# A spectral mixer on one core: 1/std applied at the point of use, no pool change ahead of half 1's first images, mixing by pairs of chunks

## The chip, the cores and the metric

The kernel runs on one core of one Trainium2 chip. The metric is the device time of one execution in microseconds (us); the median over several runs is compared. All data are float32.

## The reference, cut to what matters

The input is an image of 256 x 256 pixels with 128 channels. Layer 0 is a biased attention along the rows; its result x1 (256 tokens of 256 x 128 pixels) goes to layer 1. Layer 1 normalizes tokens, attends over them in a spectral basis, and ends with a mixer of two Fourier layers over groups of four tokens. The change concerns only the mixer:

```
h0  = instance_norm(attn)                                # attn: (64, 4, 256, 128)
h1  = fno_layer(h0, mix_wr[0], ..., norm=True, act=True)
h2  = fno_layer(h1, mix_wr[1], ..., norm=True)
out = instance_norm(h2) + attn
# fno_layer(x): skip = x mixed by a 4x4 matrix, plus a bias
#   xf = irfft2(modes(rfft2(x)) mixed by complex 4x4 weights)   32 x 16 modes
#   if norm: xf = (xf - mean(xf)) / std(xf)
#   y = xf + skip;  gelu(y) if act
```

So each Fourier layer needs the 1/std of the picture that the mixed modes make, per token. That number comes from the energy of the modes, before any picture exists.

## The kernel before, in words

The 256 tokens are worked off in two halves of 128 (a = 0 and 1), tokens or channels on the 128 partitions. A half's picture of 256 x 128 pixels is cut into 16 blocks of 2048 pixels (NB), each of two half-blocks of 1024 (HB). One half's pictures stay on chip (`blocks`, `hb[b]`); the other's go through DRAM (`yd`, `wd`).

The stages of the mixer, for each half:

- `y_blocks` (L1300 on): attention's output picture, 32 units. PE makes it (L1324, L1200), DVE takes it out of PSUM (L1334).
- `first_modes` (L1408 on): modes of the first layer. Scales the modes F, mixes them (`mix_modes`, L1341 on), and synthesizes along the height (`synth_modes`, four chunks c, matmuls at L566 or L576, copies at L584, stores of Gd1 at L589).
- `first_images` (L1452 on): for block b it loads y (L1461, half 1 only) and `gs`, the slices of Gd1 (`load_modes`, L1217, four DMAs of 64 KB). PE makes skip (L1211) and image (L1200) into the tiles `ups`, ACT applies Gelu (L1499); PE transposes the block before it (L1508), computes the statistics of the second skip (`sps`, L1211, then DVE at L1528) and the forward transform along the width (L1531), which goes to DRAM as Yd (L1534). For half 0, `add_w` also writes the residual w to DRAM (L1476 to L1480).
- `second_modes` (L1540 on): loads Yd back as YT in four chunks (L1551), transforms along the height (L1568, copies at L1574), mixes, synthesizes Gd2.
- `output` (L1614 on): per block `h2ps` = skip (L1211) and image (L1200), then ACT's Identity with scale kap and bias c0 (L1621), DVE's addition of w (L1627), and POOL's store to the output (L1628), by half-blocks.

`mix_modes` makes 16 products on DVE (L1358, each over four chunks of 128 tokens, 512 columns), which PE adds up in two PSUM tiles with an identity (L1367). Then come the squares (ACT, L1370), the energy (PE, 16 matmuls `ens`, L1376), 1/sqrt (`rsqrt`, L35 to L43: small DVE operations and one ACT square root), a diagonal (L1387) that PE spreads over all partitions (`rsp`, L1390), a copy (L1396), and two products of 512 columns that put the scaled modes into Z (L1399). Only then does `synth_modes` read Z.

The order of instructions on PE, ACT, DVE, POOL and SP is the program's own (`manual_schedule`), so it is set by Python generators: `weave` runs y_blocks between the steps of first_modes by the amounts of time that each `yield` names. At the end half 0's second modes (m0) alternate with half 1's first modes (m1); then first_images of half 1 runs with the output of half 0 woven in: in step b = 0 to 15, block c = b + 2 of half 0 is output (one step is left out on the way, by the count `due`). In such a step SP issues, in this order: y and gs of half 1's block b + 1; w and gs of half 0's block c + 1; a load that must wait for its buffer holds up all that follow it on SP.

Buffers are tiles of pools; tiles of one tag take turns in `bufs` places. Before, y and w of that stage share the tag `xt` in the pool `op0` with 4 places of 2048 pixels (L1461, L1637). The pools `op0` and `hp1` are opened when `xp` and `mp1`, used by the stages ahead, are closed, and lie over their memory.

Of the kernel before, what the change touches and what calls it, by code (L numbers as in the profile page):

```python
# [512 lines left out]
def layer1(tc, I, C, ident, x1d, upool, U, stats2, mv2, out):  # L513
# [9 lines left out]
    with ExitStack() as ctx:  # L523
# [681 lines left out]
        def skip(ps, src, blk, stop):  # L1205


            for j in range(4):
                for i in range(4):
                    r, o = slice(32 * i, 32 * i + 32), slice(32 * (i ^ j), 32 * (i ^ j) + 32)  # L1210
                    nc.tensor.matmul(rows_of(ps[j][o, :]), blk[r, r], src[r, j], start=True, stop=stop)  # L1211
# [78 lines left out]
        for a in range(2):  # L1290
            h = Half()
            halves.append(h)
            h.col = sp.tile([P, 16], FP, name=f"col_{a}")
            h.bl0 = sp.tile([P, P], FP, name=f"bl0_{a}")
            h.Gd1 = dram.tile([32, 4, 64, P], FP, name=f"Gd1_{a}")
            h.Gd2 = dram.tile([32, 4, 64, P], FP, name=f"Gd2_{a}")
            h.Yd = dram.tile([H, 32, P], FP, name=f"Yd_{a}")
# [43 lines left out]
        def mix_modes(wp, mk, psum, F, l, tag, out, constant=()):  # L1341
# [3 lines left out]
            T, G = P, P // 4  # L1345
            acc = [psum.tile(f"{tag}acc_{r}") for r in range(2)]
            by_c = [z.rearrange("p (c t) -> p c t", c=4) for z in acc]
# [5 lines left out]
            def product(k):  # L1353
                i, x, r, dst = steps[k]
                t = mk("m", [P, 4, G, 4], f"{tag}m_{k}")
                f = F[:, :, x, :].rearrange("p c (g i) -> p c g i", i=4)[:, :, :, i]
                w = mixw[r][:, :, 16 * l + 4 * i : 16 * l + 4 * i + 4]
# [4 lines left out]
            for k, (i, x, r, dst) in enumerate(steps):  # L1362
# [3 lines left out]
                yield 0.6  # L1366
                nc.tensor.matmul(acc[dst], ident, now, start=(i == 0 and x == 0), stop=(i == 3 and x == 1))  # L1367
            sq = mk("f", [P, 2, 4, T], tag + "sq")
            for r in range(2):
                nc.scalar.activation(sq[:, r], by_c[r], AF.Square)  # L1370
            yield 1.8

            en = psum.tile(tag + "ens")
            for c in range(4):
                for r in range(2):
                    nc.tensor.matmul(  # L1376
                        en[:, 0:1], sq[:, r, c, :], om0[:, min(c, 1) : min(c, 1) + 1],
# [3 lines left out]
            rs = wp.tile([P, 2], FP, tag=tag + "rs", name=tag + "rs", bufs=1)  # L1381
            rsqrt(nc, wp, rs[:, 0:1], en[:, 0:1], EPS, "rq")
            left = rs[:, 1:2]
            nc.vector.tensor_mul(left, rs[:, 0:1], rs[:, 0:1])
            nc.vector.tensor_mul(left, left, en[:, 0:1])
            dg = mk("m", [P, P], tag + "dg")
            nc.vector.tensor_scalar(dg, ident, rs[:, 0:1], None, ALU.mult)  # L1387
            yield 1.8
            ps = psum.tile(tag + "rsp")
            nc.tensor.matmul(ps[:, 0:T], ones, dg, start=True, stop=True)  # L1390
            for k, (x, m) in enumerate(constant):
                nc.tensor.matmul(
                    ps[0:1, 256 : 256 + T], x, m, start=(k == 0), stop=(k == len(constant) - 1)
                )
            rsb = mk("m", [P, T], tag + "rsb")
            nc.scalar.copy(rsb, ps[:, 0:T])  # L1396
            Z = mk("f", [P, 4, 2, T], tag + "Z")
            for r in range(2):
                nc.vector.tensor_tensor(Z[:, :, r, :], by_c[r], bc(rsb, 1, 4), ALU.mult)  # L1399
            if constant:  # L1400
                nc.vector.tensor_copy(Z[0:1, 0, 0, :], ps[0:1, 256 : 256 + T])
            else:
                nc.vector.memset(Z[0:1, 0, 0, :], 0.0)
            nc.vector.tensor_scalar(Z[0:32, 0], Z[0:32, 0], wsyn[0:32, 0:1], None, ALU.mult)
            out[:] = [Z, left]
            yield 1.8

        def first_modes(a, wp, mk, psum, gts):  # L1408
# [34 lines left out]
            z = []  # L1443

            yield from mix_modes(wp, mk, psum, F, 0, f"x{a}", z, ((sig, blk[0]), (ch[:, 2:3], ident)))
            Z = z[0]
            for c in range(4):
                synth_modes(wp, psum.pool, Z, P, h.Gd1, f"g1{a}", turned=True, chunk=c, ptag=psum.tag, gts=gts,
                            queues=(nc.gpsimd, nc.scalar))
                yield 2.7  # L1450

        def first_images(a, wp, yp, psk, pst, first=None):  # L1452
# [5 lines left out]
            def load(b):  # L1458
                if a == 1:
                    ys[b] = yp.tile([P, NB], FP, tag="xt", name=f"y2_{b}")  # L1460
# [28 lines left out]
            for b in range(17):  # L1489
# [4 lines left out]
                if b < 16:  # L1494
# [3 lines left out]
                    for j in range(4):  # L1498
                        nc.scalar.activation(by_turn(hb[b])[:, j], rows_of(ps[j]), AF.Gelu)  # L1499
# [40 lines left out]
        def second_modes(a, wp, mk, psum, gts, yts):  # L1540
# [17 lines left out]
            load(0)  # L1558
            yield 6.0
            if a:  # L1560
                load(1)
            for c in range(4):
# [12 lines left out]
                for k in ((2,), (3,), (), ())[c] if a else ((1,), (2, 3), (), ())[c]:  # L1575
                    load(k)
                if c < 3:
                    yield 4.0
            yield None
            z = []  # L1580
            yield from mix_modes(wp, mk, psum, F, 1, f"z{a}", z)
            Z, left = z
            Fw = mk("m", [P, 2, P], f"Fw_{a}")
            nc.vector.tensor_scalar(Fw, F[:, 0], hw0, None, ALU.mult)
            for c in range(4):
                if c == 2:

                    ps = psum.tile(f"cvps_{a}")
# [11 lines left out]
                yield 2.7  # L1600
# [3 lines left out]
            nc.vector.scalar_tensor_tensor(hv, ps[:, 0:1], 4.0, hv, ALU.mult, ALU.add)  # L1604
            nc.vector.tensor_add(hv, hv, left)
            rsqrt(nc, wp, kap, hv, EPS, "rq")
            nc.vector.tensor_mul(kap, kap, ch[:, 4:5])
            nc.vector.tensor_mul(c0, hm, kap)
# [5 lines left out]
        def output(a, b, gs, w, psk):  # L1614

            kap, c0 = (halves[a].col[:, k : k + 1] for k in (8, 9))
            ps = [psk.tile(f"h2ps_{a}_{b}_{j}") for j in range(4)]
            skip(ps, by_turn(hb[b]), blk[1], False)
# [334 lines left out]
```

## Time and profile before

| | us |
|---|---|
| median of 3 runs (lowest, highest) | 2897.19 (2888.25, 2899.63) |
| the profiled execution | 2898.24 |
| its span | 2896.1 |
| mean granted TensorE clock | 0.948 of full speed |

The stages of the mixer in the span, with what they kept busy:

| stage | from, to (us) | PE busy | DVE busy | DMA, GB/s |
|---|---|---|---|---|
| y_blocks, half 0 | 1903, 2043 | 138.4 | 86.4 | 277 |
| first_modes of half 0 with y_blocks of half 1 | 2043, 2190 | 128.9 | 85.7 | 284 |
| first_images, half 0 | 2190, 2332 | 134.0 | 82.9 | 310 |
| second_modes of half 0, with the last y_blocks | 2332, 2387 | 45.5 | 22.9 | 299 |
| both mixes, both syntheses | 2387, 2468 | 64.8 | 47.8 | 102 |
| first_images of half 1 with output of half 0 | 2468, 2680 | 170.8 | 107.5 | 267 to 368 |
| second_modes, half 1 | 2680, 2765 | 52.9 | 34.0 | 194 |
| output, half 1 | 2765, 2896 | 69.9 | 68.6 | 359 |

How to read it: the busy time of an engine is the sum of its instructions in the window, and a matmul's end is modelled, so a busy PE isn't PE at its peak. In the lines of a timeline the first number is the start, the second how long the group took, then engine, line, operation, output and inputs; what stands in brackets is how long the engine was idle before it, and what released it.

### The profile page before, as it was taken

The page shows a single profiled execution, that of the slowest core. Times are in us where ns is not written, and L with a number is a line of the kernel's source. Part 1 is how long each engine was busy: PE and PEld are TensorE (multiplying, and loading weights), DVE is VectorE, ACT ScalarE, POOL GpSimd, SP SyncE. Part 2 cuts the span into 40 slices and gives each one's busy share as a digit, 9 for nine tenths or more (in the row PEclk, how much of TensorE's full clock was granted, in tenths as well). Part 3 has the DMA queues.
Part 4 walks back from the last instruction along what each step waited for, and adds up shares of the span by engine and source line. Part 5 has one row for each costly group of instructions (what it writes and reads, how often), then busy time and mean ns, then how long its engine had stood idle before and what let it go on. Part 6 is the DMA issues. An engine that isn't in the chain of part 4 may idle for free. (4 is left out here: it accounts for less than half of the span.)

```text
span 2896.1 us, 70186 instructions
## 1 busy us (share of the span) xinstructions
PE 2640.4 (91%) x28524; PEld 1920.0 (66%) x28524; DVE 2007.2 (69%) x3239; ACT 1463.0 (51%) x2844; POOL 1647.4 (57%) x1282
## 2 busy tenths in 40 slices
PE   6799999999999999999999899999889987688664
PEld 6677777777777777777777656778665565354432
DVE  7788888888888888888888744756655545356445
ACT  0477777777777777777777512200004501354132
POOL 0399999999999999999999700200015721111011
PEclk9999999999999999999999999999999998799865
DMA  9421222222222222222222101188888983897598
GB/s 371 160 71 64 69 68 68 70 65 67 70 67 67 67 67 67 67 67 67 68 68 67 42 16 53 42 275 276 267 295 299 317 304 84 273 362 277 187 351 338
DMA packets 240955, 430.02 MB, mean 148 GB/s; under 512 B 26038, under 2 KB 169865, under 8 KB 232312
## 3 DMA queue, kind: packets, MB, share of 16 engines
q1 hardware_dynamic: 200184, 333.24, 34.8%
q0 software_dynamic: 23552, 83.90, 7.7%
q10 hardware_dynamic: 16896, 8.39, 1.1%
q8 instruction: 226, 3.70, 0.6%
q14 instruction: 97, 0.79, 0.1%
HBM read 290.17 MB, written 135.27 MB: 147 GB/s over the span
## 5 line engine op out<-in xcount | busy, mean ns | idle before, releaser
L299 POOL TENSOR_TENSOR e<-e,b1T 128x1024 f32<-128x1024 f32 x256 | 606.7, 2370 | 163.5 <-PE u L348 89.8
L303 POOL TENSOR_TENSOR es<-e 128x512 f32<-128x512 f32 x512 | 639.5, 1270 | 20.1
L281 ACT ACTIVATE sc<-sc,b2T 128x512 f32<-128x512 f32 x512 | 339.0, 662 | 364.6 <-PE sc L272 356.4
L323 DVE RECIPROCAL av<-av 128x256 f32<-128x256 f32 x256 | 452.3, 1767 | 27.2 <-DVE og L322 1.4
L281 ACT ACTIVATE e<-sc,b2T 128x512 f32<-128x512 f32 x512 | 348.7, 681 | 0.0
L294 DVE TENSOR_TENSOR e<-sc,b1T 128x1024 f32<-128x1024 f32 x256 | 311.0, 1215 | 0.0
L272 PE MATMUL sc<-qkT 32*128 32x256 f32 x4096 | 293.6, 400 | 1.3 <-DVE e L294 1.3
L311 PE MATMUL av<-e,v 128*32 128x256 f32 x4096 | 274.7, 385 | 0.5 <-POOL e L299 0.5
L1324 PE MATMUL yps<-xt,mpT 128*128 128x256 f32 x1024 | 244.9, 393 | 21.1 <-DVE yt L1334 12.7
L272 PEld LDWEIGHTS sc<-qkT 32*128 32x128 f32 x4096 | 185.3, 184 | 112.3 <-issue 97.8
L322 DVE SCALAR_TENSOR_TENSOR og<-gate,av 128x256 f32<-128x256 f32 x256 | 107.7, 421 | 190.6 <-PE av L316 190.6
L1324 PEld LDWEIGHTS yps<-xt,mpT 128*128 128x128 f32 x1024 | 194.5, 195 | 59.1 <-DVE yt L1334 16.3
L1338 POOL DMA_DIRECT2D yd<-yt x32 | 17.4, 545 | 346.5 <-DVE yt L1334 346.5
L327 POOL TENSOR_TENSOR x<-xt,bo 128x256 f32<-128x256 f32 x256 | 187.4, 732 | 0.0
L246 PE MATMUL qk<-xnT,wT_wq 128*128 128x256 f32 x512 | 179.5, 432 | 1.7 <-ACT xnT L238 1.7
L252 PEld LDWEIGHTS gv<-wT_wv,kvT 128*128 128x128 f32 x1024 | 155.0, 192 | 13.4
L316 PE MATMUL av<-es,ones 128*32 128x256 f32 x2048 | 157.5, 379 | 2.6 <-POOL es L303 2.5
L333 PE MATMUL wo<-wT_wo,og 128*128 128x128 f32 x1024 | 156.8, 276 | 2.7 <-DVE og L324 2.7
L1621 ACT ACTIVATE blocks<-h2ps,col 128x512 f32<-128x512 f32 x128 | 89.0, 777 | 138.5 <-PE h2ps L1200 130.2
L311 PEld LDWEIGHTS av<-e,v 128*32 128x32 f32 x4096 | 107.0, 109 | 76.1 <-POOL e L299 1.0
L348 PE MATMUL u<-adft,x 128*128 128x129 f32 x1024 | 156.4, 275 | 0.0
L252 PE MATMUL gv<-wT_wv,kvT 128*128 128x128 f32 x1024 | 156.0, 275 | 0.0
(524 smaller groups left out, 5204.6 us busy)
## 6 DMA issues: line engine op xcount, KB each, us to landing
xt<-x1d SPq DMA_DIRECT2D x128, 512.0 KB
xb<-in_x_dram SPq DMA_DIRECT2D x32, 1024.0 KB
xt<-in_x_dram SPq DMA_DIRECT2D x128, 256.0 KB
kt<-in_L_conv_kv_x_dram SPq DMA_DIRECT2D x128, 256.0 KB
x1d<-x SPq DMA_DIRECT2D x256, 128.0 KB
gs<-Gd SPq DMA_DIRECT2D x384, 64.0 KB
yd<-yt POOLq DMA_DIRECT2D x32, 512.0 KB, 5.7
xw<-x1d SPq DMA_DIRECT2D x32, 512.0 KB
```

Source lines behind the costliest of these rows:

```text
L246: nc.tensor.matmul(ps[:, 0:256], wT["wq"], xnT, start=True, stop=True)
L252: nc.tensor.matmul(ps[:, 256 + c * P : 256 + (c + 1) * P], kvT[:, c * P : (c + 1) * P], wT["wv"], start=True, stop=True,)
L272: nc.tensor.matmul(sc[h // 2][:, h % 2, c * 256 : (c + 1) * 256], qkT[p, 256 + c * P : 256 + (c + 1) * P], qkT[p, 0:256], start=True, stop ...
L281: nc.scalar.activation(r["e"][1][:, :, c, :] if hp else z, z, AF.Exp, bias=b2T[:, c, s : s + 1])
L294: nc.vector.tensor_tensor(r["e"][0].rearrange("p h c q -> p (h c q)"), r.pop("sc").rearrange("p h x -> p (h x)"), b1T[:, 0:2].rearrange("p ...
L299: nc.gpsimd.tensor_tensor(e1, e1, b1T[:, 2:4].rearrange("p h c q -> p (h c q)"), ALU.mult)
L303: nc.gpsimd.tensor_tensor(r["es"][hp], e[:, :, 0, :], e[:, :, 1, :], ALU.add)
L311: nc.tensor.matmul(ps[hd, 0:256], r["v"][:, c, hd], r["e"][h // 2][:, h % 2, c, :], start=(c == 0), stop=(c == 1),)
L316: nc.tensor.matmul(ps[32 * h : 32 * h + 32, 256:512], self.ones, r["es"][h // 2][:, h % 2, :], start=True, stop=True,)
L323: nc.vector.reciprocal(rd, rd)
L327: nc.gpsimd.tensor_tensor(r["x1"], r["x"], bc(self.bo, 1, 2), ALU.add)
L1324: nc.tensor.matmul(rows_of(ps[j]), mpT[:, sc, tt], by_turn(xt[:, sc])[:, j], start=(sc == 0), stop=False,)
```

## The change

- `mix_modes` now takes the accumulators and a list of chunks `cs`, and mixes only these. `mixed` copies the unscaled sums into Z (ACT one, DVE the other) and takes the squares. `norm` computes 1/std later and leaves it as a column (`h.col[:, 12:13]`) and as a row spread over the partitions (`h.row`). Synthesis starts from the unscaled Z; `norm` is called after the chunks 0 and 1.
- What made up for that: for the first layer, the scale and the constant go into Gelu as its scale and bias (`h.turn`, one pair of columns for each of the four turned orders j), and the skip's blocks `h.bl0` are divided by the 1/std. For the second, `h.bl0` becomes the skip's blocks divided by it (four operations), and `krs`, the product of kap and 1/std, is Identity's scale.
- `second_modes` transforms the chunks 0 and 1, mixes them, with the transforms of chunks 2 and 3 inside this mix, and then mixes the chunks 2 and 3. Half 1's first modes are stepped along with both.
- The pool `op0` is gone. `hp1` is opened inside `xp`'s context, so `xp` stays. y of half 1 has three places in `xp`'s `xt` of its own. w of half 0, from block 2 on, is loaded by half-blocks: half-block k goes to `hp1`'s single place `wx` if k is a multiple of 3, else to one of the two places `yt` of `xp`.
- The pool of half 1's output, `op1`, is on the right side of memory.

```diff
@@ skip
-    nc.tensor.matmul(rows_of(ps[j][o, :]), blk[r, r], src[r, j], start=True, stop=stop)
+    w = blk[r, r] if len(blk.shape) == 2 else blk[r, j]
+    nc.tensor.matmul(rows_of(ps[j][o, :]), w, src[r, j], start=True, stop=stop)
...
+def mixed(mk, acc, tag):
+    by_c = [z.rearrange("p (c t) -> p c t", c=4) for z in acc]
+    Z = mk("f", [P, 4, 2, P], tag + "Z")
+    nc.scalar.copy(Z[:, :, 0, :], by_c[0])
+    nc.vector.tensor_copy(Z[:, :, 1, :], by_c[1])
+    nc.vector.memset(Z[0:1, 0, 0, :], 0.0)
+    nc.vector.tensor_scalar(Z[0:32, 0], Z[0:32, 0], wsyn[0:32, 0:1], None, ALU.mult)
+    sq = [mk("m", [P, 4, P], f"{tag}sq_{r}") for r in range(2)]
+    for r in range(2):
+        nc.scalar.activation(sq[r], by_c[r], AF.Square)
+    return Z, sq
...
@@ norm
-    rsb = mk("m", [P, T], tag + "rsb")
-    nc.scalar.copy(rsb, ps[:, 0:T])
-    Z = mk("f", [P, 4, 2, T], tag + "Z")
-    for r in range(2):
-        nc.vector.tensor_tensor(Z[:, :, r, :], by_c[r], bc(rsb, 1, 4), ALU.mult)
+    nc.vector.scalar_tensor_tensor(left, en[:, 0:1], EPS, rs, ALU.add, ALU.mult)
+    nc.vector.tensor_scalar(dg, ident, left, None, ALU.mult)
...
@@ first_modes, after each chunk of synthesis
+    if c == 0:
+        yield next(tail)
+        yield next(tail)
+    if c == 1:
+        run(tail)
+        nc.vector.tensor_mul(h.bl0, h.bl0, h.row[:, 0:P])
+        ps = h.row
+        nc.tensor.matmul(ps[:, 256:257], blk[0], sig, start=True, stop=False)
+        nc.tensor.matmul(ps[:, 256:257], ident, ch[:, 2:3], start=False, stop=True)
+        nc.vector.tensor_copy(h.col[:, 13:14], ps[:, 256:257])
+        turned = mk("m", [P, 4, P], f"turned_{a}")
+        for j in range(4):
...
+            nc.tensor.matmul(ps[:, 260 + 2 * j : 262 + 2 * j], turned[:, j], h.col[:, 12:14], start=True, stop=True)
+        nc.vector.tensor_copy(h.turn, ps[:, 260:268])
...
@@ first_images
-    ys[b] = yp.tile([P, NB], FP, tag="xt", name=f"y2_{b}")
+    ys[b] = yp.tile([P, NB], FP, tag="xt", name=f"y2_{b}", bufs=3)
...
-    nc.scalar.activation(by_turn(hb[b])[:, j], rows_of(ps[j]), AF.Gelu)
+    nc.scalar.activation(
+        by_turn(hb[b])[:, j], rows_of(ps[j]), AF.Gelu,
+        bias=h.turn[:, 2 * j + 1 : 2 * j + 2], scale=h.turn[:, 2 * j : 2 * j + 1],
+    )
...
@@ second_modes
+    forward(0)
+    load(2 if a else 1)
+    yield 4.0
+    forward(1)
...
+    mix = mix_modes(mk, acc, F, 1, f"z{a}", range(0, 2))
+    for k, t in enumerate(mix):
+        if k in (2, 10):
+            forward(2 + k // 8)
+        yield t
     yield None
-    yield from mix_modes(wp, mk, psum, F, 1, f"z{a}", z)
+    yield from mix_modes(mk, acc, F, 1, f"z{a}", range(2, 4))
+    Z, sq = mixed(mk, acc, f"z{a}")
...
@@ output
-    skip(ps, by_turn(hb[b]), blk[1], False)
+    skip(ps, by_turn(hb[b]), by_blocks(halves[a].bl0), False)
...
@@ output_0, load(b)
-    t = wp.tile([P, NB], FP, tag="xt", name=f"w_{b}", bufs=bufs)
-    nc.sync.dma_start(t, wd[:, b * NB : (b + 1) * NB])
-    gs = gp.tile([P, 4, P], FP, tag="gs", name=f"gs3_0_{b}", bufs=3 if gp is xp else 2)
+    if b < 2:
+        t = xp.tile([P, NB], FP, tag="xt", name=f"w_{b}", bufs=3)
+        nc.sync.dma_start(t, wd[:, b * NB : (b + 1) * NB])
+        t = [t[:, 0:HB], t[:, HB:]]
+    else:
+        t = []
+        for k in (2 * b, 2 * b + 1):
+            tag = (pools[0], "wx", 1) if k % 3 == 0 else (xp, "yt", 2)
+            t.append(tag[0].tile([P, HB], FP, tag=tag[1], name=f"w_{b}_{k}", bufs=tag[2]))
+            nc.sync.dma_start(t[-1], wd[:, k * HB : (k + 1) * HB])
+    gs = xp.tile([P, 4, P], FP, tag="gs", name=f"gs3_0_{b}", bufs=3)
     load_modes(gs, halves[0].Gd2, b)
...
@@ the driver
-    for _ in range(3):
-        next(m1)
-    run(iter(lambda: next(m0), None))
+    next(m1)
+    for k, _ in enumerate(iter(lambda: next(m0), None)):
+        if k % 4 == 3:
+            next(m1)
     for _ in m0:
-        next(m1)
-    pools = [xp, xp, 3, True]
+        next(m1, None)
+    pools = [None]
...
-with tc.tile_pool(name="op0", bufs=4) as op, tc.tile_pool(name="hp1", bufs=2) as wp:
-    pools[:] = [op, wp, 4, True]
-    for done in first_images(1, wp, op, bq, br, (y2, g2)):
+    with tc.tile_pool(name="hp1", bufs=2) as pools[0]:
+        next(o0)
+        next(o0)
+        for done in first_images(1, pools[0], xp, bq, br, (y2, g2)):
...
-with tc.tile_pool(name="op1", bufs=2) as op:
+with tc.tile_pool(name="op1", bufs=2, side="right") as op:
```

## The prediction

> **What bounds the kernel now.** I began with the page. The chain that ended last gives layer 1's lines only small shares, and the change touches only layer 1, from 1903 us to the end. So I asked for the busy time of each engine by stage, over windows cut where the groups begin and end:
>
> ```profile
> 2468.00:2520.00 52.00, 32.33 (x406) 15.51 (x395) 10.42 (x12) 15.32 (x24) 4.72 (x8) 0.65 0.78 267
> 2520.00:2560.00 40.00, 34.75 (x689) 19.63 (x684) 24.81 (x34) 22.30 (x38) 7.32 (x12) 0.96 0.96 333
> 2560.00:2600.00 40.00, 35.24 (x699) 18.96 (x699) 25.36 (x36) 23.03 (x39) 6.25 (x10) 1.00 1.02 368
> ```
>
> The columns are window, length, PE, PEld, DVE, ACT, POOL, granted clock, DMA share, GB/s. From 2520 us on, first_images(1) runs with output_0 woven in, with DMA full and PE nearly so: neither has room, and no engine waits long. The 52 us before it are another matter: PE at a clock of 0.65, DMA not full. The timeline of SP, whose program order is fixed, tells why, and how a steady step goes:
>
> ```profile
> 2495.95 0.34 SPq L1461 DMA_DIRECT2D y<-yd  x1
> 2496.46 3.31 SPq L1217 DMA_DIRECT2D gs<-Gd  x4
> 2499.81 0.42 SPq L1637 DMA_DIRECT2D w<-wd  x1
> 2500.27 4.03 SPq L1217 DMA_DIRECT2D gs<-Gd  x4
> ...
> 2557.44 0.34 SPq L1461 DMA_DIRECT2D y<-yd  x1
> 2557.87 3.99 SPq L1217 DMA_DIRECT2D gs<-Gd  x4
> 2561.96 1.07 SPq L1637 DMA_DIRECT2D w<-wd  x1
> 2563.07 3.97 SPq L1217 DMA_DIRECT2D gs<-Gd  x4
> ```
>
> The first four lines are loads for blocks 1 and 2. They come 10 us after SP's previous issue, and block 2's image then waits until 2508.09 us, because y_1 sits in a pool laid over memory whose last store must land. The last four are one step: y and gs of half 1, then w and gs of half 0. SP's waits say what stops it:
>
> ```profile
> SPq L1461 <- DMA out_dram<-w: 41.0, 12, 10.6
> SPq L1637 <- DMA Gd<-g11gt: 9.3, 3, 5.7
> ```
>
> So already now a load waits 12 times for the store of an output, since y and w share four buffers. What hides most of that is that w of block c+1 is issued a whole block ahead. In the timeline of all engines, block 7 of half 0 (output of block c = b + 2 in step b = 5):
>
> ```profile
> 2562.04 1.17 PE L1200 MATMUL h2ps<-k_bsyn,gs 32*128 32x128 f32 x32
> 2563.24 2.79 ACT L1621 ACTIVATE blocks<-h2ps,col 128x512 f32<-128x512 f32 x4 [1.60 <-PE h2ps L1200]
> 2564.28 2.49 DVE L1528 BATCH_NORM_STATS2 hstat<-sps 128x6 f32<-128x512 f32 x4 [2.71 <-PE sps L1211]
> 2566.68 2.35 DVE L1627 TENSOR_TENSOR w<-w,blocks 128x1024 f32<-128x1024 f32 x2
> 2568.19 0.53 POOL L1628 DMA_DIRECT2D out_dram<-w  x1 [0.39 <-DVE w L1627]
> ```
>
> The w of block 8 was issued at 2561.96, six microseconds before the first half of block 7 is even stored at 2568.19.
>
> **What the skill says.** "DMA: Bandwidth & Descriptors", Anatomy of one DMA: a semaphore wait happens on the issuing sequencer before dispatch, not in the DMA engines. The trace agrees: SP stood up to 10.6 us at L1461, and the loads behind it stood too. The same section gives some 2.0 us plus bytes over 436 GB/s for a transfer, an estimate of 3.2 us for 512 KB; traces differ with load: 3.5 us where little else moved (store issued 2492.42, load released 2495.95), 5.7 us for yd on the page, 8.9 us median for out_dram in 2520 to 2680. "ScalarE: Activation LUTs", What ACT_TABLE_LOAD costs: each per-partition pointer operand adds about 93 ns. It agrees: 603 ns for Gelu (L1499, none), 777 ns for L1621 (two), 174 ns apart. "TensorE: Matmul & The Clock Gate", Part 1: the PE clock falls when PE idles; agrees in kind with 0.65 above.
>
> **The change, part by part.**
>
> **(1) The 1/std applied later.** In half 0's second mix, the chain from the last accumulation to the first synthesis runs from 2425.7 (ens) to 2432.17 (first g20): 16 matmuls, square root, diagonal, broadcast, two 0.65 us products. After, only one 0.6 us copy on ACT beside one 0.7 us on DVE, a memset 0.17 and a scaling 0.34 stand there, 1.8 us: 4.7 off. Half 1's Z, ready at 2444.5 because its chain queued behind g20, is ready some 15 us sooner, so PE can alternate g20 and g11 from the start; they now take 2432.2 to 2468.6 = 36.4 us for 8 chunks. Three buffers for 8 chunks stay, at about 8.5 us each (evacuation 1.3, issue 2, landing 5): not below 23 us. I take 4 us off besides the 4.7: 9 in all, from 5 to 15. In the first mix of half 0 the chain lies among y_blocks, which fill PE (128.9 of 147 us): 0. The added 4 turns, small matmuls and copies there (about 2 us per half) lie beside that, and for half 1 beside the buffer wait; if that cover is gone they cost 2. Gelu gains 4 x 0.17 us a block: ACT has 23 busy of 40 us in half 1's stage and 74 of 142 in half 0's, where it also waits 37 us for stores of yA: 0, at most 0.7 x 16 = 11 if ACT were the bound. Output's scaled blocks (L1211) are as many matmuls of the same size: 0.
>
> **(2) Mixing by pairs.** A product of 512 columns takes 0.69 us on DVE and 0.86 on PE; half of it about half (0.36 and 0.43, estimated from the size). In the second mix of half 0, pair 0 moves into half 1's chain of small operations (2388.6 to 2394.7), but DVE then does in sequence what it did with gaps: 16 x 0.36 more. PE's remaining 16 x (0.43 + 0.86) = 20.6 us starts at about 2403.5 and ends at 2424, as now (2424.9): 0 to 2, inside the 9. In half 1, where YT lands from 2688 to 2703, mixing now starts at 2706.7 and Z is ready at 2731; pair 0 in the wait for YT saves 5, the norm 5, together 10. DVE's adds of the output ahead (each waits for a load) stand before the copies of chunks 1 and 2 now, so 3 come back: 7 off, 3 to 10. Output 1 is DMA-bound at 359 GB/s, so its end moves with its start. The pool on the other side moves no issue: y and x ahead are queued behind YT (2695.5): 0.
>
> **(3) No change of pools.** y_1, w_2 and their gs can follow gs2_1_0 (issued until 2485) without the 10 us on SP: 10 off, 6 to 13. With (1), half 0's block 2 reaches its image evacuation at 2510.4 - 19 = 2491.
>
> **(4) What pays for it: half-blocks of w.** w from block 2 has three half-block buffers (yt two, wx one): half k takes the place of k - 3. Block c+1 is halves 2c+2 and 2c+3, and 2c+3 replaces 2c, **the first half of block c**. SP issues it ahead of gs of c+1, y of b+2 and gs of b+2, so all of these are queued behind a wait for block c's own store to land. PE's image of c+1 waits for that gs, in order, with sps and ups behind it. This is a loop of one block, with nothing ahead:
> image end to store issue 5.0 us (2563.21 to 2568.19); landing 5.7 (between 3.5 and 8.9; the yd row, whose stage moved some 285 GB/s, is the nearest); w issue 0.35; four gs issues 2.1 (1.82 to 4.0); landing of the last 2.9 (2.0 to 3.8, the last from 2504.3 to 2508.09); rest of the image 1.0. Sum **17.0 us**, from 13.3 (all low, 0.6 for the image) to about 20 (landings cannot stay at 8.9 when 3.93 MB move in 17 us, 231 GB/s).
> Now the evacuations of block 2 and block 15 stand at 2510.44 and 2659.81: 149.4 us for 13 intervals, one of them a double step that the weaving skips. After: 13 x 17.0 = 221 us (in the skipped step the two steps' work of about 17 fits too). That is +71.6.
>
> **Sum.** +71.6 - 9 - 10 - 7 = +45.6. Against the profiled execution's 2898.24 us (span 2896.1) this is 2943.8; the median of the runs is 1.05 lower, so 2943.
>
> **Rivals.**
> *A, faster: the store is waited for, but other work covers it.* For it: now too SP waits 41 us for such stores and DMA still runs at 1.0; y has three buffers of its own, so that wait goes. Against: y is not what block c+1's image needs next; gs is, and it is behind the wait. If the interval stayed at 10.7 to 11.5, 2898 - 26 + 0 to 10 = 2872 to 2882. It decides below 13.5 us an interval ((149.4 + 26) / 13).
> *B, no change: the loop is real but at its shortest.* At 13.3 us, 13 x 13.3 = 173, +23.5 - 26: 2896. For it: with 295 GB/s the DMA is less full and landings shorten.
> *C, slower still: PE's clock falls in the waits.* In 2468 to 2520 skips took 3.4 to 3.9 us instead of 1.2. If sps and the image take 2 to 3 us more, 20 us an interval: +110.6 - 26, 2983.
> *D: the pool gain is not there*, because gs2 of half 1 lies in the new pool over mp1, whose y2_0 is read by block 0's skip: 10 of the 26 lost, 2953, inside the forecast.
>
> **How the numbers follow.** Forecast with D 0.64, C 0.06, B 0.14, A 0.16. A measurement of this kernel tells about 0.5% (14.5 us) from no change. Slower by more: forecast and C, 0.70; within: B, 0.14; faster: A, 0.16. The forecast's own range is 2912 to 2975. Taking in B and most of A below, and C's 2983, the range is 2868 to 2985.
>
> **What would show it.** In the profile after: w loads (two per block, 512 KB) that wait for out_dram, nearly one per block and several us each; evacuations of h2ps some 17 us apart from block 2 to 15; DMA share near 0.65 and a lower PE clock in that stage; y_1's issue within a few us of gs2_1_0's; g20 starting about 2 us after the last z0acc; z1's products starting before 2700 on the old scale. I am wrong if the intervals stay below 13.5 us, or if gs of c+1 is found issued before the store of block c has landed.

## The result and the profile after

The kernel after takes **2979.12 us** (median of 4 runs, 2965.81 to 2983.64), the kernel before 2893.53 in the runs beside it (4 runs, 2888.25 to 2899.63): ratio 1.0287, 95% interval [1.0244, 1.0331], slower. The profiled execution has a span of 2973.1 us at a mean clock of 0.941, 77.0 us longer than the span of before. The budget below is made from these two executions.

First the windows that the prediction showed, now of the kernel after (window, length, busy PE, PEld, DVE, ACT, POOL, granted clock, DMA share, GB/s):

```profile
2468.00:2520.00 52.00, 35.89 (x698) 20.97 (x698) 15.76 (x36) 19.10 (x29) 8.58 (x14) 0.84 0.83 287
2520.00:2560.00 40.00, 30.37 (x416) 15.34 (x432) 13.28 (x18) 14.08 (x22) 3.65 (x6) 0.73 0.67 233
2560.00:2600.00 40.00, 30.52 (x440) 11.83 (x408) 17.39 (x24) 15.81 (x24) 4.12 (x7) 0.76 0.64 219
```

The stage that was full is no longer so: DMA 0.67 and 0.64 instead of 0.96 and 1.02, PE's clock 0.73 and 0.76 instead of 0.96 and 1.00. In the first window the clock is higher (0.84 instead of 0.65), but the two windows don't hold the same work: half 0's first Identity stands at 2492.17 in it and stood at 2477.92 before. Next, SP's timeline (start, duration of the group) at the start of the stage, and two of its steps:

```profile
2497.91 1.15 SPq L1705 DMA_DIRECT2D w<-wd  x2
2499.11 2.38 SPq L1221 DMA_DIRECT2D gs<-Gd  x4
2501.59 0.43 SPq L1490 DMA_DIRECT2D y<-yd  x1
...
2522.75 11.67 SPq L1705 DMA_DIRECT2D w<-wd  x2
2534.48 2.01 SPq L1221 DMA_DIRECT2D gs<-Gd  x4
2536.59 1.39 SPq L1490 DMA_DIRECT2D y<-yd  x1
2538.08 1.77 SPq L1221 DMA_DIRECT2D gs<-Gd  x4
2539.96 13.97 SPq L1705 DMA_DIRECT2D w<-wd  x2
2553.97 1.92 SPq L1221 DMA_DIRECT2D gs<-Gd  x4
```

y_1 (2501.59) now follows its neighbours without a gap: the 10 us stop for the laid-over pool is gone. But each pair of w's halves takes SP 10 to 14 us (12.22, 11.67, 13.97, 10.43 and 13.20 in the five rounds from 2505.78 on), since the second one stands at a wait, and gs, y and gs stand behind it. SP's waits (line, what it waited for, sum, times, longest):

```profile
SPq L1705 <- DMA out_dram<-w: 148.9, 13, 16.0
```

Before it was 41.0 in 12 waits. One round of the loop, from the timeline of all engines (the store of block c, then the image of block c+1):

```profile
2541.47 2.78 ACT L1682 ACTIVATE blocks<-h2ps,col 128x512 f32<-128x512 f32 x4 [5.71 <-PE h2ps L1200]
2543.77 2.49 DVE L1560 BATCH_NORM_STATS2 hstat<-sps 128x6 f32<-128x512 f32 x4 [8.83 <-PE sps L1212]
2546.18 2.34 DVE L1688 TENSOR_TENSOR w<-w,blocks 128x1024 f32<-128x1024 f32 x2
2548.16 1.20 POOL L1689 DMA_DIRECT2D out_dram<-w  x2
...
2553.59 0.34 SPq L1705 DMA_DIRECT2D w<-wd  x1
2553.97 1.92 SPq L1221 DMA_DIRECT2D gs<-Gd  x4
2555.94 0.42 SPq L1490 DMA_DIRECT2D y<-yd  x1
...
2557.52 1.92 PE L1200 MATMUL h2ps<-k_bsyn,gs 32*128 32x128 f32 x32 [3.78 <-DMA gs<-Gd]
2559.18 2.78 ACT L1682 ACTIVATE blocks<-h2ps,col 128x512 f32<-128x512 f32 x4 [6.09 <-PE h2ps L1200]
```

Store issued at 2548.16; w's second half goes at 2553.59, when it has landed; four gs; PE waits 3.78 us for them. From evacuation to evacuation 17.71 us.

**Where 77.0 us come from.** Five marks in each trace: the load of F for half 1, the start of half 0's second synthesis (g20; its Z is ready then), the first Identity of half 0 (L1621, later L1682), that of blocks 2 and 15, and the first Identity of half 1.

| stretch | before | after | change | predicted |
|---|---|---|---|---|
| up to the load of F | 2387.40 | 2392.67 | +5.3 | 0 |
| to half 0's Z | 44.8 | 49.4 | +4.6 | -9 with the next |
| synthesis, to half 0's first Identity | 45.8 | 50.1 | +4.3 | |
| to block 2 | 32.5 | 17.8 | -14.8 | -10 |
| blocks 2 to 15 | 149.4 | 226.3 | +76.9 | +71.6 |
| to half 1's first Identity | 99.9 | 99.2 | -0.7 | -7 |
| the rest | 136.4 | 137.7 | +1.3 | 0 |

The loop alone is the whole loss; what was to pay a part of it back came only in the startup. Even there it only made up for what had been lost ahead: block 2 is evacuated at 2509.92, before at 2510.44, where the prediction had 2491. These are two questions: whether the loop is what the prediction says (e3, e1, e6), and where the arithmetic's gain went (the other runs).

### The profile page after: what moved, and what is told of

Its sections match the earlier page's. It is cut to its first block, busy times and chain, and to the rows that moved or that the text cites. A ratio compares the mean times of both kernels' runs of the same rounds, so it can differ in the third digit from the quotient of the medians.

```text
span 2973.1 us, 70394 instructions
## 1 busy us (share of the span) xinstructions
PE 2680.2 (90%) x28604; PEld 1938.5 (65%) x28604; DVE 2015.8 (68%) x3297; ACT 1484.6 (50%) x2844; POOL 1646.6 (55%) x1282
## 5 line engine op out<-in xcount | busy, mean ns | idle before, releaser
L272 PEld LDWEIGHTS sc<-qkT 32*128 32x128 f32 x4096 | 185.6, 184 | 112.4 <-issue 97.8
L1343 POOL DMA_DIRECT2D yd<-yt x32 | 17.4, 545 | 349.9 <-DVE yt L1339 349.9
L1200 PE MATMUL h2ps<-k_bsyn,gs 32*128 32x128 f32 x1024 | 86.6, 387 | 103.7 <-DMA gs<-Gd 96.5
L1682 ACT ACTIVATE blocks<-h2ps,col 128x512 f32<-128x512 f32 x128 | 89.0, 777 | 179.4 <-PE h2ps L1200 179.4
L1200 PEld LDWEIGHTS h2ps<-k_bsyn,gs 32*128 32x128 f32 x1024 | 74.2, 269 | 146.7 <-DMA gs<-Gd 122.8
```

The costliest lines, as they stand in the source:

```text
L272: nc.tensor.matmul(sc[h // 2][:, h % 2, c * 256 : (c + 1) * 256], qkT[p, 256 + c * P : 256 + (c + 1) * P], qkT[p, 0:256], start=True, stop ...
L1200: nc.tensor.matmul(ps[j][:, k * W : (k + 1) * W], gs[q, n, :], bs[q, :], start=False, stop=(k == len(rows) - 1),)
```

## The experiments

The same stretches, in us, for every kernel (F as its time):

| kernel | F | to Z | synthesis | to block 2 | 2 to 15 | to half 1's Identity |
|---|---|---|---|---|---|---|
| before | 2387.4 | 44.8 | 45.8 | 32.5 | 149.4 | 99.9 |
| after | 2392.7 | 49.4 | 50.1 | 17.8 | 226.3 | 99.2 |
| e3, before with w's halves | 2385.7 | 45.2 | 45.8 | 30.8 | 232.1 | 94.8 |
| e1, after, modes ahead of w | 2398.4 | 51.5 | 53.7 | 23.5 | 181.1 | 104.7 |
| e5, e1 without half 0's pairs | 2393.0 | 39.0 | 49.5 | 24.0 | 181.3 | 102.6 |
| e6, e5, w's second half later | 2396.0 | 39.4 | 49.3 | 23.7 | 161.8 | 97.9 |
| e9, e6, adds later | 2398.4 | 39.4 | 49.9 | 23.1 | 160.7 | 98.7 |
| e4, after in the pools of before | 2392.5 | 50.5 | 50.7 | 27.8 | 155.1 | 100.1 |
| e12, e4, small operations first | 2389.5 | 47.7 | 50.3 | 30.8 | 155.9 | 98.9 |
| e7, e4 without pairs | 2389.2 | 39.3 | 50.7 | 29.4 | 152.3 | 99.6 |
| e8, e7 without the factor | 2388.3 | 38.5 | 51.0 | 30.5 | 148.3 | 103.7 |
| e10, e7, norm behind the chunks | 2391.7 | 39.2 | 46.5 | 33.9 | 153.4 | 96.3 |
| e11, e10, adds behind too | 2395.1 | 39.0 | 46.4 | 32.8 | 154.2 | 108.3 |
| e13, e10, first_modes of before | 2388.0 | 38.5 | 50.4 | 33.1 | 150.7 | 97.8 |

One profile each: after, e1, e4 and e7 share their code up to F, and stand at 2389.2 to 2398.4 there, so a difference of a few us in one row proves nothing; what all rows of one kind agree on says more.

### Is it the loop? e3, e1, e6

**e3** is the kernel before with part 4 alone (y keeps three places for itself):

```diff
-t = wp.tile([P, NB], FP, tag="xt", name=f"w_{b}", bufs=bufs)
-nc.sync.dma_start(t, wd[:, b * NB : (b + 1) * NB])
+t = []          # from block 2 on
+for k in (2 * b, 2 * b + 1):
+    t.append(wp.tile([P, HB], FP, tag="wx", name=f"w_{b}_{k}", bufs=3))
+    nc.sync.dma_start(t[-1], wd[:, k * HB : (k + 1) * HB])
```

> The kernel before with part (4) alone: from block 2 on w comes by half-blocks with three places of its own, y keeps three places; everything else as before. Loop theory: the same loop as in the changed kernel, 17 us an interval from block 2 to 15, so 226 us instead of 149, total about 2893 + 75 = 2968. Arithmetic theory: as before, 2893. Half-load theory: also some 2968, so this run parts it from the loop only together with the run that issues gs first.

Measured 2973.69 us, ratio 1.029 [1.0255, 1.0325], that of the whole change. SP's waits in it:

```profile
SPq L1644 <- DMA out_dram<-w: 157.5, 13, 14.8
```

Thirteen waits again, 17.9 us an interval. Part 4 is enough for the loss, without any of the other parts.

**e1** is the kernel after with the four gs loads of a block issued ahead of its w halves:

```diff
+gs = xp.tile([P, 4, P], FP, tag="gs", name=f"gs3_0_{b}", bufs=3)
+load_modes(gs, halves[0].Gd2, b)
 for k in (2 * b, 2 * b + 1):
 ...
-gs = xp.tile([P, 4, P], FP, tag="gs", name=f"gs3_0_{b}", bufs=3)
-load_modes(gs, halves[0].Gd2, b)
```

> The changed kernel with one thing moved: in output_0 the four gs loads of a block are issued on SP ahead of its two half-blocks of w, not behind them. Loop theory (the image of block c+1 waits for gs that stands behind a wait for block c's store): the loop of one block opens; what stays behind the wait is y and gs of half 1's block b+2, needed two steps on, so (5.7 landing + 0.4 + 5 y landing + 12 from ups to the next store) / 2 = 11.5 us an interval. Evacuations of h2ps from block 2 to 15 then take some 150 us instead of 226, total about 2979 - 76 = 2903. Arithmetic theory (Gelu's two operands, the turned columns, the scaled skip are what costs): nothing changes, 2979. Half-load theory (two loads of 512 KB instead of one of 1 MB, and DMA's handling of them, cost): nothing changes, 2979.

Measured 2944.03, ratio 1.0171 [1.0132, 1.021]: half of the way. The interval is 13.9 us, not 11.5. It fell although the half-blocks, their stores and the arithmetic stayed as they were, so none of these explains the part that fell. In SP's timeline of e1:

```profile
2567.02 6.46 SPq L1709 DMA_DIRECT2D w<-wd  x2
2573.53 1.86 SPq L1490 DMA_DIRECT2D y<-yd  x1
```

PE's:

```profile
2566.73 1.15 PE L1212 MATMUL ups<-y,bl 32*32 32x512 f32 x32 [0.54 <-DMA y<-yd]
...
2581.92 2.02 PE L1212 MATMUL ups<-y,bl 32*32 32x512 f32 x32 [5.00 <-DMA y<-yd]
```

gs of half 0 got past the wait, but y of half 1 is still behind it, and PE now waits for y: the loop is shorter, not open.

**e6** (on e5, below) issues the second half one step later, behind the gs of the block after:

```diff
 load_modes(gs, halves[0].Gd2, b)
+if b > 2:
+    half(b - 1, 2 * b - 1)     # w's half k into the ring
+half(b, 2 * b)
```

> The kernel with the modes of the output's half 0 ahead of its w halves and half 0's Z without pairs (2926.47 us, 13 intervals of 13.9 us), with one more edit: the second half of a block's w is issued one step later, behind the modes of the block after, so that the store that has to land before it is a step older. Theory (SP's queue stands at the second half's wait, and half 1's modes and y stand behind it): the intervals of blocks 2 to 15 fall to 11.0 to 11.5 us, SP's wait for w's stores falls from 12 us per block to under 3, and the time to about 2926 - 13 x 2.6 = 2892 us. Rival (the stores and loads themselves are the limit, whatever their order; three half places are too few): intervals stay at 13.5 or more, 2920 or more.

Measured 2906.81, ratio 1.0038 [1.0026, 1.005], against e5's 1.0116 [1.0082, 1.015]. SP's waits in e6:

```profile
SPq L1721 <- DMA out_dram<-w: 28.2, 16, 6.5
```

ACT's:

```profile
2528.53 2.79 ACT L1690 ACTIVATE blocks<-h2ps,col 128x512 f32<-128x512 f32 x4 [1.76 <-PE h2ps L1200]
2538.67 2.79 ACT L1690 ACTIVATE blocks<-h2ps,col 128x512 f32<-128x512 f32 x4 [1.76 <-PE h2ps L1200]
2553.57 2.79 ACT L1690 ACTIVATE blocks<-h2ps,col 128x512 f32<-128x512 f32 x4 [1.80 <-PE h2ps L1200]
```

The wait fell from 71.0 us (e5) to 28.2 with the same three places, the same bytes and the same stores; steps of 10.14 us appear, where before has 9.4 to 10.9 in most. The DMA share from 2520 to 2660 is 0.94 again. So what cost most of the 77 us is not that there are half-blocks, nor how many, but the place of loads in an in-order queue: gs put ahead (e1) and one half put later (e6) together bring the stretch from 226.3 us to 161.8. Not all is back: the interval is 12.4 us, between the expected 11.0 to 11.5 and the rival's 13.5, and 161.8 us stand against 149.4. A part of that isn't the loop's (the Gelu, below). And some steps still take 14 us: in the one that ends at 2553.57 PE waits 2.4 us for y, and DVE 7.5 us for w's late half.

### Where did the arithmetic's gain go? e4, e5, e12, e7, e8

**e4** is the kernel after with parts 3 and 4 undone (the pools, y and w as before; the pool of half 1's output on the left again).

> The changed kernel with parts (3) and (4) undone: pools op0 and hp1 over released memory, y and w sharing four places of a block, output's pool on the left side again; the later 1/std and the mixing by pairs stay. From the budget of the two traces: up to half 1's F load +5, mixes and syntheses +9, second_modes and output of half 1 +3, and no loop: 2893 + 17 = 2910. Loop theory: intervals about 10.7 to 11.5 again. Arithmetic theory: intervals stay at 17, total about 2979.

Measured 2917.78, ratio 1.0098 [1.0066, 1.0131]. The loop is gone here too (155.1 us), and what is left is a loss where the prediction had a gain.

**e5** is e1 with half 0's pairs undone: four forwards, then one mix of four chunks, and half 1's small operations in three steps ahead of it, as before.

> The kernel with gs first, and with mixing by pairs undone in half 0's second layer only: chunks 2 and 3 are transformed ahead, half 1's first three steps run ahead, then four chunks are mixed together with half 1's mix, as in the kernel before. If the pairs there cost time because DVE, PE and ACT wait for one another in program order inside the chain of small operations (24.5 us from the first product to the last of pair 0, where the chain alone took 9), Z of half 0 comes 10 us sooner after the F load and the total is 6 to 10 below the kernel with gs first. If PE's work is what counts there (the prediction's view), the two are alike within 2 us.

Measured 2926.47, ratio 1.0116 [1.0082, 1.015], 17.6 us below e1: more than expected. Half 0's Z comes 39.0 us after F instead of 51.5.

**e12** is e4 with only the order undone, pairs kept:

```diff
-next(m1)
-for k, _ in enumerate(iter(lambda: next(m0), None)):
-    if k % 4 == 3:
-        next(m1)
+for _ in range(3):
+    next(m1)
+run(iter(lambda: next(m0), None))
```

> The arithmetic of the change in the pools of before (2917.78 us), pairs kept in both halves, with half 1's first small operations taken in three steps ahead of half 0's pairs, as the kernel before has them, instead of one for every four steps of the pairs. Theory A (the interleaving in program order is what costs: DVE and PE wait in turn for the small operations' chain): half 0's Z is ready 39 to 42 us after the load of F instead of 50, and the time is some 2905 us. Theory B (the pairs themselves cost, as half-size products with as long an interlock): Z stays at 47 to 51 us, 2914 us or more.

Measured 2909.77, ratio 1.0058 [1.0036, 1.0079]; Z at 47.7 us, so theory B: of the 11 us up to Z the order is worth some 3, the pairs themselves the rest. (The time fell by more than these 3 us, below B's 2914; F's load stands 3 us earlier too, and the rest I can't place.) DVE's timeline of e12, in the first and the second pair:

```profile
2404.66 0.42 DVE L1362 TENSOR_TENSOR z0m<-F,mixwi 128x256 f32<-128x256 f32 x1 [0.36 <-PE z0acc L1371]
...
2405.88 0.42 DVE L1362 TENSOR_TENSOR z0m<-F,mixwr 128x256 f32<-128x256 f32 x1 [0.36 <-PE z0acc L1371]
...
2425.61 0.43 DVE L1362 TENSOR_TENSOR z0m<-F,mixwn 128x256 f32<-128x256 f32 x1 [0.26 <-PE z0acc L1371]
2425.95 0.68 DVE L1362 TENSOR_TENSOR x1m<-F,mixwr 128x512 f32<-128x512 f32 x1
2426.90 0.42 DVE L1362 TENSOR_TENSOR z0m<-F,mixwi 128x256 f32<-128x256 f32 x1 [0.26 <-PE z0acc L1371]
```

And of e7:

```profile
2410.03 0.69 DVE L1362 TENSOR_TENSOR z0m<-F,mixwr 128x512 f32<-128x512 f32 x1 [0.42 <-PE z0acc L1371]
2410.64 0.68 DVE L1362 TENSOR_TENSOR x1m<-F,mixwn 128x512 f32<-128x512 f32 x1
2411.75 0.69 DVE L1362 TENSOR_TENSOR z0m<-F,mixwr 128x512 f32<-128x512 f32 x1 [0.42 <-PE z0acc L1371]
```

Without pairs a whole z0 product and a whole x1 product share 1.72 us. With pairs the first 16 halves run without x1 (two of them in 1.22 us, and two forwards, 2 to 2.6 us each, among them: 2397.9 to 2412.1). Then the driver alternates the streams step by step, as before, so that each half of the second pair has a whole x1 product beside it: 1.29 us a step (2425.61 to 2426.90). Counted in the two timelines, 15 products of x1 stand ahead of Z's copy in e12, and 15 in e7: that half of z0 was done early spares Z none of them. (This is read from the order; no run moved x1's products behind.) From z0's first product to Z's copy e7 takes 29.4 us (2397.80 to 2427.20), e12 38.0 (2397.89 to 2435.93).

**e7** is e4 with the pairs undone in both halves, so the later 1/std alone.

> The arithmetic of the change (1/std later) in the pools of before (2917.78 us), with the pairs undone in both halves: what is left of the change is the later 1/std alone. Theory A (the pairs inside the chain of small operations cost 18 us in half 0, and the later 1/std is worth little on its own): 2900 us, half 0's Z ready 12 us earlier after the load of F. Theory B (what that kernel lost lies in the turned diagonals, the Gelu's operands and the later factor): 2912 us or more.

Measured 2910.15, ratio 1.0052 [1.0027, 1.0078]. Theory A's place is right: Z 11.2 us earlier than in e4. Its sum isn't: by the ratios to before 0.46%, 13 us, below e4 instead of 18, between A and B. (Its five runs lie apart, two near 2899 and three near 2911; the profiled one is the fastest, so its row stands for the fast ones.) And its row shows the second leak: Z is ready 5.5 us earlier than before, the synthesis takes 4.9 longer.

**e8** is e7 with plain Gelu and without the turned diagonals; it leaves out the normalization's factor and constant in the first images.

> The kernel of the later 1/std alone, with the turned diagonals, their matmuls and copies, and the Gelu's scale and bias operands left out; this leaves out the normalization's factor and constant from the first images. The difference to the kernel with them prices the factor's new place. Theory A (the chain of turned diagonals holds PE and DVE in the stage of y's second half, +5 us up to the first ups, the Gelu's 0.7 us a block is hidden): 5 us below the kernel with them. Theory B (hidden as forecast): within 2 us of it. Theory C (the Gelu's operands cost their 16 x 0.7 us too): 16 us below it.

Measured 2900.43, ratio 1.0035 [1.0023, 1.0046]; the spans of the two profiled executions are equal (2895.7), the medians 10 us apart (5 by the ratios). By column: the load of F stands at 2385.7 to 2388.3 in the four kernels without the turned chain (before, e3, e8, e13) and at 2389.2 to 2398.4 in the ten with it; blocks 2 to 15, in the kernels with the loads of before, take 148.3 to 150.7 without the Gelu's operands (before, e8, e13) and 152.3 to 155.9 with them (e4, e7, e10, e11, e12). In half 0's first images ACT is busy 85.6 us in e7 and 74.1 in e8, but from the first Gelu to the last it is 122.7 and 120.5 us, within the 120.2 to 125.3 of all fourteen kernels: hidden there, as forecast. In half 1's stage it isn't, and ACT's timelines show how much. Before:

```profile
2520.66 2.79 ACT L1621 ACTIVATE blocks<-h2ps,col 128x512 f32<-128x512 f32 x4 [1.76 <-PE h2ps L1200]
2525.78 2.06 ACT L1499 ACTIVATE blocks<-ups 128x512 f32<-128x512 f32 x4 [1.60 <-PE ups L1200]
2530.08 2.79 ACT L1621 ACTIVATE blocks<-h2ps,col 128x512 f32<-128x512 f32 x4 [1.76 <-PE h2ps L1200]
```

e7:

```profile
2520.19 2.78 ACT L1680 ACTIVATE blocks<-h2ps,col 128x512 f32<-128x512 f32 x4 [1.76 <-PE h2ps L1200]
2525.31 2.78 ACT L1528 ACTIVATE blocks<-ups,turn 128x512 f32<-128x512 f32 x4 [1.61 <-PE ups L1200]
2530.32 2.78 ACT L1680 ACTIVATE blocks<-h2ps,col 128x512 f32<-128x512 f32 x4 [1.76 <-PE h2ps L1200]
```

The step is 9.42 us before and 10.13 in e7, and the Gelu's 0.72 us are the whole difference: Identity, ups, Gelu and h2ps follow one another with the same waits, although ACT was busy only 23 of 40 us before. PE's skip behind the Gelu, h2ps, takes 2.14 us in that step instead of 1.42. The shortest steps are 9.41 to 9.42 us in before, e8 and e13, and 10.09 to 10.14 in the kernels with the operands where the loop doesn't hold them; e6's 10.14 are these. In longer steps a part of the 0.72 us is covered. So the factor's new place costs some us at two places, and e8's later column (103.7) takes a part back; a closer number for the whole these runs don't give.

### Giving the synthesis back: e10, e9, e11, e13

**e10** is e7 with norm's operations, the skip's blocks and the weights of the mean put behind the four chunks of second_modes:

```diff
 for c in range(4):
     synth_modes(...)
     yield 2.4
-    if c == 0:
-        yield next(tail)
-        yield next(tail)
-    if c == 1:
-        run(tail)
-        ...
+yield next(tail)
+yield next(tail)
+run(tail)
+...
```

> The kernel of the later 1/std alone (no pairs, pools of before: 2910.15 us, its profiled execution 2897.5), with all that hangs on 1/std in second_modes (the sums of squares, the root, the row, the skip's blocks, and the weights of the mean behind them) put behind the four chunks of the synthesis instead of between them. Theory (the small operations between the chunks hold PE and DVE: start of the synthesis to half 0's first Identity 50.7 us instead of 45.8, half 1's synthesis 29 us instead of 17, and what was gained ahead of the synthesis is spent there): 45 to 46 us and 17 to 20 us again, 8 to 13 us below that kernel. Rival (behind the chunks the chain to the output's scale becomes the last one to arrive, and the first outputs wait for it as long): within 3 us of that kernel.

Measured 2896.16, ratio 1.0014 [1.0, 1.0028], by the ratios 11 us below e7. In half 0 the synthesis takes 46.5 us instead of 50.7: the theory's size. But block 2 gains nothing from it: the stretch behind takes 33.9 us instead of 29.4. These kernels keep the pools of before, and y_1, which waits there, is issued at 2499.58 in e10 and at 2497.35 in e7. The spans of the two profiled executions are alike too (2895.8 and 2895.7), so the traces don't place the 11 us between the medians. In half 1 its stores are issued up to 20.4 us after its start (29.1 in e7), but half 1's first Identity comes only 3.3 us earlier by the last column, since the rival has a share there: the chain behind the chunks is the last to arrive. In e10's timeline:

```profile
2745.61 1.49 POOL L589 DMA_DIRECT2D Gd<-g21gt  x2 [2.91 <-DVE g21gt L584]
...
2757.53 1.45 PE L1212 MATMUL h2ps<-blocks,bl 32*32 32x512 f32 x32 [1.53 <-DVE col L1656]
```

**Half 1's adds.** In half 1 the synthesis of after takes 29 us (2794.17 to the last store's issue at 2823.32) instead of 17. DVE's timeline of before:

```profile
2734.90 1.29 DVE L584 COPY g21gt<-g21gp 128x512 f32<-128x512 f32 x2 [1.85 <-PE g21gp L566]
2736.10 1.28 DVE L1674 SCALAR_TENSOR_TENSOR x<-y,col,x 128x1024 f32<-128x1024 f32 x1
2737.74 1.29 DVE L584 COPY g21gt<-g21gp 128x512 f32<-128x512 f32 x2 [0.36 <-PE g21gp L566]
```

After:

```profile
2796.26 1.29 DVE L584 COPY g21gt<-g21gp 128x512 f32<-128x512 f32 x2 [0.79 <-PE g21gp L566]
2797.47 1.28 DVE L1742 SCALAR_TENSOR_TENSOR x<-y,col,x 128x1024 f32<-128x1024 f32 x1
2800.90 1.28 DVE L1742 SCALAR_TENSOR_TENSOR x<-y,col,x 128x1024 f32<-128x1024 f32 x1 [2.15 <-DMA x<-x1d]
2807.18 1.28 DVE L1742 SCALAR_TENSOR_TENSOR x<-y,col,x 128x1024 f32<-128x1024 f32 x1 [2.83 <-DMA x<-x1d]
2808.39 1.28 DVE L584 COPY g21gt<-g21gp 128x512 f32<-128x512 f32 x2
```

Between one chunk's copies and the next on DVE (1.55 us apart in before, 10.8 in after) stand adds that wait for x (5.0 us of waits), and norm's chain among them. **e9** starts these adds four steps later in e6 (`k >= 20` for `k >= 16`), **e11** puts them behind all second modes in e10.

> The kernel with w's second half late, with half 1's adds of x and y begun four steps later, once two of the four chunks of the synthesis are issued. Theory (DVE's adds, which wait for x, stand ahead of the chunk's copies: the synthesis took 29 us instead of 17): 8 to 12 us below the kernel with w's second half late, about 2882 us. Rival (the adds only fill idle time, the synthesis is bound by its own PE, ACT and store steps): within 3 us of it, the adds then late for the first outputs.

> The same, and half 1's adds of x and y put behind its second modes altogether. Theory (the adds' waits for x stand ahead of the chunks' copies on DVE): a further 2 to 5 us below. Rival (the adds are then late for the first outputs): 0 to 6 us above.

e9: 2903.07, ratio 1.0028 [1.0017, 1.004], 3.7 us below e6, at the rival's edge and far from the 8 to 12 expected. Its stores end 22.5 us after the synthesis's start instead of 28.3, but a later add waits 6.25 us for x in front of the output's constants. e11: 2913.76, ratio 1.0075 [1.0054, 1.0096], some 18 us above e10, three times the rival's most. SP's timeline of e11 tells why:

```profile
2766.63 0.32 SPq L1719 DMA_DIRECT2D y<-yd  x1
2766.99 0.43 SPq L1723 DMA_DIRECT2D x<-x1d  x1
2767.74 5.86 SPq L1221 DMA_DIRECT2D gs<-Gd  x8
```

PE's:

```profile
2773.59 2.53 PE L1200 MATMUL h2ps<-k_bsyn,gs 32*128 32x128 f32 x32 [15.70 <-DMA gs<-Gd]
```

The adds free the places of y, SP's next loads wait for that, and the first output's gs stand behind these loads: the same figure as in the loop. For the synthesis itself the runs divide the 12 us: norm and what hangs on it behind the chunks gives 8.7 back (e7 to e10, 29.1 to 20.4), the adds behind too another 5.4 (e10 to e11, 15.0); the adds alone gave 5.8 (e6 to e9).

**e13** is e10 with first_modes and Gelu as before.

> The kernel with 1/std behind the chunks of second_modes (2896.16 us, 1.0014 of before), with first_modes and the Gelu as the kernel before has them, so that the later 1/std stands in the second modes alone. Theory (half 0's Z 5.5 us earlier at no price behind it, and the turned diagonals and the Gelu's operands, which cost 4 to 5 us up to the load of F, gone): 5 to 8 us below that kernel, 2885 to 2891, so some 0.1 to 0.3% faster than before. Rival (the small operations of first_modes now stand ahead of half 1's synthesis, which runs beside half 0's on the same DVE and ACT, and hold its stores): as that kernel or slower, 2896 or more.

Measured 2892.34, ratio 1.0 [0.9986, 1.0013]: 3.8 us below e10's median, between the theory's 2885 to 2891 and the rival's 2896, and not faster than before. Z comes 38.5 us after F, but the synthesis takes 50.4 again: in this kernel half 1's norm stands before its synthesis, beside half 0's, which fits the rival; no run parts it from other causes. No version that I made beats the kernel before; norm behind the chunks together with the new pools (e6 with e10) was not tried.

## Why the prediction was right, and where its sum failed

- **The loop (part 4)**: right in mechanism, and shown (e3 makes it alone; e1 and e6 take 64.5 of its 76.9 us away by the order of loads alone, apart from half 0's pairs, which leave this stretch as it is: 181.1 and 181.3). Its terms, in the round above: image to store 6.7 us (5.0 predicted; the statistics of sps, L1560, run before the add), landing 5.4 (5.7), w's issue 0.4, gs issues 1.9 (2.1), last landing and rest of the image 3.3 (3.9): 17.7 against 17.0. The 13 intervals took 226.3 instead of 221, and that lies in one place: the double step (2657.57 to 2686.15) took 28.6 us, not the 17 that I gave it, and the other twelve 16.5 each.
- **Startup (part 3)**: -14.8 against -10; rival D is out. The stop at y_1 is gone, as said. How much of it is the pools' is not parted by a run of its own: the kernels in the pools of before take 27.8 to 33.9 there, those in the new ones 17.8 to 24.0.
- **Later 1/std in half 0**: the 4.7 us ahead of Z are there (e7: 5.5). The step that failed is the "4 us off besides": synthesis grew by 4.3, because the operations taken from ahead of it now stand between its chunks on the same DVE and PE. e10 gives 4.2 of it back by order alone (though not to block 2, see there). I had priced what left the chain and not where it went.
- **Pairs in half 0**: "0 to 2, inside the 9" failed; e4 against e7 has 11.2 us up to Z. I counted DVE's and PE's work, which is nearly the same, and not the alternation with half 1's mix: 15 of its products stand ahead of Z with pairs and without, so the early half added 14 us in front (e12) and spared less behind.
- **First modes, the Gelu's operands**: "0", with 2 if the cover is gone. The trace shows PE in the turned chain waiting 2.6 us for DVE (L1464); F's load is 5.3 later. In half 0's images the operands are hidden, as said. In half 1's stage the "0" failed: ACT's share of busy time was no measure of it, since ACT and PE wait for each other in turn there, and the shortest steps are longer by the full 0.72 us (e7); over blocks 2 to 15 that is some 3 us.
- **Half 1's second modes**: Z is 13 us sooner (58.0 us after block 15's Identity instead of 71.3; 10 predicted), but the "3 come back" was mis-sized: 12 came back, and the adds, which I had named, are the smaller part of it (5 to 6); the new place of norm and of what hangs on it, which I had not priced, is the larger (8.7, e10). The pairs have no share in the gain: from block 15's Identity to the synthesis e4 takes 59.3 us, e7 without pairs 58.7.
- **Rivals**: A and B are out by the interval of 17.4. C's clock is there (0.76) and its interval isn't: skips take 2.0 us instead of 1.2, and the round is still 17.7 us, not 20.

So the cause was right and the sum was not: of the three gains (9, 10 and 7 us) only the 10 came. 2943 was 36 us short of the median after, which lies above the forecast's own 2912 to 2975; that it is still inside the range given is owed to C's 2985 at its upper end, and C is not what happened. The profiles' 77.0 minus the predicted 45.6 are 31.4, of which 5.3 are the loop, 5.3 the first modes, 17.9 half 0's Z and synthesis, 6.3 half 1's second modes, 1.3 the output, and -4.8 the startup (rounded).

## What to carry to other kernels

When a buffer ring gets shorter than the distance at which its loads are issued, look for what is queued behind the waiting load on the in-order engine: the price is the whole loop from store to next image, and moving the waiting loads behind their neighbours can return most of it. When small operations are moved out of a chain, write down between which instructions of which engine they now stand: between the chunks of half 0's synthesis they cost most of what they had saved (4.9 of 5.5 us, e7), behind the last chunk next to nothing of that stretch (46.5 us instead of 45.8, e10). A low share of busy time doesn't make an engine's work free where it and another wait for each other in turn. And where two streams are woven step by step, count how many steps of the other one stand ahead of the end of the one that is wanted: here an early start did not change that count.

## What I had not expected

- One load moved by one step, with the same bytes and buffers, was worth some 20 us (e5 to e6: intervals of 13.9 to 12.4 us).
- The Trainium skill says that the PE clock is throttled after idle time and released by activity ("TensorE: Matmul & The Clock Gate", Part 1). The traces agree in kind: from 2520 to 2680 the mean granted clock was 0.73 to 0.86 in the windows of after, where PE waits in each step, and with the loop opened it stood at 0.94 (e6, 2520 to 2660; before 0.98).
